# A hybrid attention kernel: its hand-set task slots replaced by a list scheduler, with attention tiles as filler

## The chip, the core and the metric

The kernel runs on one core of a Trainium2 chip. The core has a matrix engine (TensorE, PE in the profile), a vector engine (VectorE, DVE), a scalar engine (ScalarE, ACT), GpSimd (POOL) and SyncE (SP), which here issues nearly all the DMAs. Each engine works through its own instruction queue in order; semaphores tie the queues together. The metric is the device time of one execution in microseconds (us). The kernel before took 2002.72 us, the median of 3 runs from 1999.59 to 2007.79.

## The reference, cut to what matters

Everything is float32. The input is a batch of 4 images of 56 x 56 positions with 128 channels. Two layers follow each other.

```python
# layer 0: 7x7 neighbourhood attention with 4 heads of 32 channels
y    = group_norm(x)                        # 32 groups, statistics over a whole image
q,k,v = split(y @ qkv_w.T + qkv_b)
attn = softmax(q . k_window / sqrt(32) + rel_bias)   # 49 keys of each query
x    = x + (attn . v_window) @ proj_w.T + proj_b
# layer 1, on the 3136 tokens of an image
t = x.reshape(B, 3136, 128)
n = layer_norm(t)
q, k, v = exp(n @ Wq), exp(n @ Wk), n @ Wv
t = t + q @ (k.T @ v)                       # needs the sum over all tokens first
n = layer_norm(t)
t = t + spectral_filters(n) + sum(shift(n, i) @ M_u[i] for i in range(3))
```

Three dependences matter. The normalisation of layer 0 needs a whole image's statistics. The product `k.T @ v` needs every token of an image, so the second half of layer 1 starts when the last attention row of the image has passed through the first half. The spectral filters need whole images again.

## The kernel before

The program has three parts. `layers` does layer 0 and the start of layer 1. `spectral_layer` does the filters and `onto_the_rest` adds the result to the output. A second version of everything (`general`) runs only if the attention sums leave a safe range; with these inputs it does not. Only `layers` is changed.

In `layers` an image is cut into 7 rows of 8 x 56 positions, and each row into 5 query tiles (four of 96 queries and one of 64): 140 tiles for 4 images. One tile does this:

```python
def score_keys(n):                # 16 small matmuls -> 4 PSUM banks, one buffer (pool ps_s)
    t["sp"] = pools["ps_s"].tile([P, NH, 512], F32, tag="s", name="sp")
    for c in range(2):
        for h in range(NH):
            nc.tensor.matmul(t["sp"][:kn, h, c*nq:(c+1)*nq], keys_of(...)[hs], qTs[b, ty][hs, ...])

def exponentials(n):              # bias added by DVE out of PSUM, exponential by ACT in SBUF
    nc.vector.tensor_tensor(e, t["sp"][:kn, :, : 2 * nq], relb[...], ALU.add)
    nc.scalar.activation(e, e, AF.Exp)

def weigh_keys(n):                # 32 small matmuls -> half of 1 PSUM bank, one buffer (ps_o)
    t["po"] = pools["ps_o"].tile([P, 2, NQ], F32, name="po")
    for i in range(2):            # i = 0: weighted values, i = 1: the sum of the weights
        for c in range(2):
            for h in range(NH):
                nc.tensor.matmul(t["po"][hs, i, :nq], ones[:kn] if i else t["v"][:kn, c, hs], t["e"][:, h, c])

def collect_keys(n):              # DVE: reciprocal of the sums, then the product
    nc.vector.reciprocal(rec, po[:, 1, :nq])
    nc.vector.tensor_tensor(aT, po[:, 0, :nq], rec, ALU.mult)
```

All other work is written as tasks (Python generators): `group_stats` and `group_norm`, `keys`, `queries`, `values`, `mix` (projection and first half of layer 1 of a row), `products` (the 128 x 128 product of an image), `finish` (second half of a row), `row_transforms` (start of the filters), `filter_transforms` and `filter_matrices`. They share the 3 PSUM banks that the attention leaves. The main loop places them between the steps of the tiles, at tile numbers written by hand, and a task may ask to be left alone for a number of slots (`late`):

```python
for b in range(B):
    n0 = b * PER                                   # PER = 35 tiles an image
    for k in range(2, NCH):
        at(n0 + 5 * (k - 1) - 4, heads_of, b, k)   # values, queries, keys of a row
    ...
    for k in range(NCH):
        at(n0 + 5 * k + 8, lambda b, k: start(mix(b, k)), b, k)
        n1 = n0 + PER + 8
        at(n1 + (5 * k) // 2 if b + 1 < B else n0 + PER + 5, lambda b, k: start(finish(b, k)), b, k)
    ...
while n < N + behind or tasks or any(m >= n for m in plan):
    ...
    exponentials(n)
    weigh_keys(n - 1)
    slot()                        # every waiting task makes one step if a bank is free
    collect_keys(n - 1)
    score_keys(n + 1)
    slot(); slot(); slot()
    n += 1
```

The layer norm of a row, used twice a row (in `mix` and in `finish`):

```python
def normalized(acc, hn):
    for g in range(4): nc.vector.bn_stats(stats[:, g, :], acc[...])
    ...                           # 5 small DVE operations on 112 x 4 values
    nc.gpsimd.tensor_scalar(...)  # 4 small POOL operations, one a power of -0.5
    for g in range(4):            # the normalisation itself, on POOL
        nc.gpsimd.tensor_scalar(hn[...], acc[...], rstd[...], shift[...], ALU.mult, ALU.add)
```

## Time and profile before

The profiled execution spans 2005.2 us. The engines' busy time over the whole span:

| engine | busy us | share | what it does most |
|---|---|---|---|
| PE | 1746.0 | 87% | matmuls of the filters |
| PE weight loads | 1312.5 | 65% | beside the matmuls |
| DVE | 1055.1 | 53% | copies out of PSUM, attention |
| ACT | 728.2 | 36% | copies out of PSUM, exponentials |
| POOL | 346.4 | 17% | layer norms, only in the first part |

The shares are averages over parts with different limits, so the profile is best read by part. The first part (`layers`) ends where the first matmul that writes `pg` starts, at 942.4 us. Its operations for one attention tile of 96 queries, as they are on the engines:

| operation | engine | one of 96 queries (median) | all 140 tiles |
|---|---|---|---|
| scores (`sp`), 16 matmuls | PE | | 111.8 us |
| bias added (`e<-sp,relb`) | DVE | 950 ns | 125.9 us |
| exponential (`e<-e`) | ACT | 842 ns | 111.9 us |
| weighted values and sums (`po`), 32 matmuls | PE | | 162.4 us |
| reciprocal (`recs<-po`) | DVE | 748 ns | 99.6 us |
| product (`aT<-po,recs`) | DVE | 257 ns | 35.1 us |

In a view of stages every line has the stretch in us from the start of the span, its length, then for each engine the busy us and (in brackets) the number of instructions, then the granted TensorE clock as a share of full speed, the DMA share and the GB/s. In a view of waits a line names the engine, the output and the line of code that waited, then what it waited for, then the us in total, the number of times and the longest.

### The profile page before, as it was taken

What the parts mean: (1) busy time and instruction counts of PE and PEld (TensorE: products, weight loads), DVE (VectorE), ACT (ScalarE), POOL (GpSimd) and SP (SyncE); (2) the same over time, 40 slices, a digit from 0 to 9 for tenths busy, and PEclk for the clock granted to TensorE, in tenths of its full rate; (3) what the DMA queues carried; (4) which work ended last, traced back from release to release, by engine and by line L of the source; (5) the groups of instructions that cost most, each with busy time, mean ns of one, the idle gap of its engine ahead of it and who ended that gap; (6) DMA issues with size and microseconds to landing.
All of it is one profiled execution on the core that took longest, in us unless ns stands there. A gap on an engine that the chain in (4) does not pass through costs nothing.

```text
span 2005.2 us, 69052 instructions
## 1 busy us (share of the span) xinstructions
PE 1746.0 (87%) x30641; PEld 1312.5 (65%) x30641; DVE 1055.1 (53%) x2242; ACT 728.2 (36%) x1431; POOL 346.4 (17%) x626
## 2 busy tenths in 40 slices
PE   3787877988888878875999999999999999996798
PEld 2565655756665666552888888888888888884121
DVE  2666656565656555331555555555555555552232
ACT  2243322343234323313444444444444444442000
POOL 7125324532453242140000000000000000000000
PEclk7788788888788878775899999999999999998555
DMA  4553543342223223237144443444434434343986
GB/s 102 114 113 76 112 100 103 86 123 73 75 83 108 68 60 87 79 103 196 39 92 102 90 110 85 102 107 90 111 84 106 102 84 102 86 88 92 242 217 184
DMA packets 281239, 209.33 MB, mean 104 GB/s; under 512 B 102243, under 2 KB 250115, under 8 KB 280803
## 3 DMA queue, kind: packets, MB, share of 16 engines
q1 hardware_dynamic: 274266, 191.97, 39.7%
q10 hardware_dynamic: 6664, 12.85, 2.3%
q8 instruction: 243, 3.98, 0.8%
q14 instruction: 66, 0.53, 0.1%
HBM read 117.10 MB, written 87.64 MB: 102 GB/s over the span
## 4 chain that ended last, share of the span: by engine, by line
PE 50%; DMA 5%; POOL 1%; DVE 1%; issue 1%; ACT 0%; SPq 0%; ACTq 0%; POOLq 0%; DVEq 0%
PE pg L1329 19%; PE py L1349 18%; PE po L1456 3%; PE px L1310 2%; DMA z<-zd 2%; PE xx L1310 2%; PE xx L1374 2%; PE px L1374 2%; DMA out_dram<-tl 2%; PE be L736 1%; DMA v<-vd 1%; PE bk L736 0%; PE bk L688 0%; POOL hn L440 0%; POOL v L431 0%
## 5 line engine op out<-in xcount | busy, mean ns | idle before, releaser
L1339 DVE COPY gt<-pg 128x448 f32<-128x448 f32 x672 | 388.4, 620 | 344.3 <-PE pg L1329 344.3
L1339 ACT COPY gt<-pg 128x448 f32<-128x448 f32 x672 | 326.8, 540 | 396.4 <-PE pg L1329 376.7
L1329 PE MATMUL pg<-v,mats 32*128 32x112 f32 x10752 | 401.3, 285 | 22.4 <-DMA xm<-xd 12.0
L1329 PEld LDWEIGHTS pg<-v,mats 32*128 32x128 f32 x10752 | 340.1, 190 | 108.7 <-issue 98.2
L1349 PE MATMUL py<-gt,us 128*32 128x128 f32 x9408 | 373.6, 293 | 3.5 <-ACT ys L168 1.4
L1349 PEld LDWEIGHTS py<-gt,us 128*32 128x32 f32 x9408 | 299.8, 145 | 36.4 <-issue 2.7
L989 ACT ACTIVATE e<-e 126x768 f32<-126x768 f32 (+1 forms) x140 | 111.9, 799 | 225.7 <-DVE e L983 225.5
L969 PE MATMUL sp<-qT,kp 32*126 32x96 f32 (+1 forms) x2240 | 111.8, 319 | 61.5 <-DVE e L983 60.5
L969 PEld LDWEIGHTS sp<-qT,kp 32*126 32x126 f32 (+1 forms) x2240 | 87.3, 212 | 94.8 <-DVE e L983 64.0
L1456 PE MATMUL po<-z,onto 84*56 84x512 f32 x224 | 126.0, 1066 | 22.5 <-DMA z<-zd 22.5
L983 DVE TENSOR_TENSOR e<-sp,relb 126x768 f32<-126x768 f32 (+1 forms) x140 | 125.9, 900 | 27.2 <-PE sp L969 26.4
L1019 DVE RECIPROCAL recs<-po 128x96 f32<-128x96 f32 (+1 forms) x140 | 99.6, 712 | 66.9 <-PE po L1001 66.5
L1001 PE MATMUL po<-e,v_sb 126*32 126x96 f32 (+1 forms) x2240 | 82.4, 270 | 42.1 <-DVE aT L1020 22.0
L1456 PEld LDWEIGHTS po<-z,onto 84*56 84x56 f32 x224 | 31.8, 207 | 116.6 <-issue 99.0
L1001 PEld LDWEIGHTS po<-e,v_sb 126*32 126x32 f32 (+1 forms) x2240 | 50.7, 120 | 86.5 <-issue 48.0
L1465 DVE SCALAR_TENSOR_TENSOR tl<-po,hmask,tl 56x512 f32<-56x512 f32 x56 | 42.0, 750 | 107.3 <-PE po L1456 99.5
L688 PE MATMUL bk<-mu,ut 128*112 128x128 f32 x624 | 79.2, 287 | 9.7 <-ACT ut L682 7.3
L430 POOL TENSOR_SCALAR v<-v 112x4 f32<-112x4 f32 x56 | 11.2, 199 | 431.3 <-DVE v L429 429.6
L688 PEld LDWEIGHTS bk<-mu,ut 128*112 128x112 f32 x624 | 75.7, 193 | 12.1 <-ACT ut L682 9.4
L1001 PE MATMUL po<-e,ones 126*32 126x96 f32 (+1 forms) x2240 | 80.0, 266 | 0.0
L698 DVE SCALAR_TENSOR_TENSOR acc<-bk,tmask,acc 112x128 f32<-112x128 f32 x104 | 29.3, 344 | 94.1 <-PE bk L688 71.1
L404 PE MATMUL bk<-ident,hna 112*128 112x112 f32 x108 | 40.6, 424 | 30.3 <-POOL hna L440 29.8
(196 smaller groups left out, 2116.7 us busy)
## 6 DMA issues: line engine op xcount, KB each, us to landing
xd<-xs SPq DMA_DIRECT2D x112, 168.0 KB
xm<-xd SPq DMA_DIRECT2D x84, 224.0 KB
yd<-ys SPq DMA_DIRECT2D x168, 112.0 KB
yg<-yd SPq DMA_DIRECT2D x84, 224.0 KB
zd<-zs SPq DMA_DIRECT2D x84, 224.0 KB
z<-zd SPq DMA_DIRECT2D x14, 1344.0 KB
v_sb<-vpad SPq DMA_DIRECT2D x224, 63.0 KB
acc<-in_x_dram SPq DMA_DIRECT2D x28, 224.0 KB
```

Of the source, the lines that this page charges most:

```text
L688: nc.tensor.matmul(pt[:CP, g * C : (g + 1) * C], ut[:, t0 : t0 + 2 * CP - 1 : 2], mu[:, i, :], start=(i == 0), stop=(i == NAR - 1),)
L969: nc.tensor.matmul(t["sp"][:kn, h, c * nq : (c + 1) * nq], keys_of(x0, y0 + c * KH, KH)[hs], qTs[b, ty][hs, QR * x0 : QR * x0 + nq], start ...
L983: nc.vector.tensor_tensor(e.rearrange("k (h q) -> k h q", h=NH), t["sp"][:kn, :, : 2 * nq], relb[tiles[n][3]].rearrange("k h c q -> k h (c ...
L989: nc.scalar.activation(e, e, AF.Exp)
L1001: nc.tensor.matmul(t["po"][hs, i, :nq], ones[:kn] if i else t["v"][:kn, c, hs], t["e"][:, h, c], start=(c == 0), stop=(c == 1),)
L1019: nc.vector.reciprocal(rec, po[:, 1, :nq])
L1310: nc.tensor.matmul(pu[:, b].rearrange("p c m -> p (c m)"), xm[:, s, b, :], tables_of(m1)[1], start=True, stop=True,)
L1329: nc.tensor.matmul(pg[g // 2][g % 2][:, 2 * N2 * i : 2 * N2 * (i + 1)], mats[rows, 4 * n + i, :], v[rows], start=True, stop=True,)
L1339: copy(gt[:, h, :, e0 : e0 + 4, :], pg[q][h][:, : 8 * N2].rearrange("p (i m c) -> p m i c", i=4, c=2),)
L1349: nc.tensor.matmul(py[32 * j : 32 * (j + 1), slot, :], us.rearrange("p c k m -> p (c k) m")[:, NSB * (1 - c) : NSB * (5 - c), m2], gt[:, : ...
L1374: nc.tensor.matmul(pz, tables_of(m1)[2], yg[:, s * B : (s + 1) * B].rearrange("p k e -> p (k e)"), start=True, stop=True,)
L1456: nc.tensor.matmul(po[64 * q : 64 * q + H].rearrange("p b c -> p (b c)"), onto[:, s], zin[q][:, i, s], start=(s == 0), stop=(s == NS - 1),)
```

## The change

The hand-set slots go. In their place the Python code that writes the program keeps a rough clock for each engine. Every task declares before each step whether the step uses PE and how many PSUM banks it needs, and after the step how long its engines will take (`use`). `go()` picks the next step: one whose inputs are ready by that clock, steps without PE first, then by rank. The attention tiles become tasks themselves, with the worst rank (9), so that they fill the time in which no other step is ready; three of them may be under way (`AHEAD`). SyncE's DMAs are now issued in the order in which the scheduler writes them; before, only the four compute engines had a fixed order. The clock is only used to choose the order: on the chip the semaphores decide.

```diff
+            def use(*choices):
+                engine, cost = min(choices, key=lambda c: max(busy[c[0]], at[0]) + c[1])
+                busy[engine] = max(busy[engine], at[0]) + cost
+                at[0] = busy[engine] + HOP                       # HOP = 0.2
+                return engine
 ...
+            def go():
+                now = busy["PE"]
+                for t in tasks:
+                    tensor, need, gate = t[3]
+                    ready = gate() if gate else 0.0
+                    if ready is None or need > len(banks):
+                        continue
+                    ready = max([ready, t[4]] + sorted(banks.values())[:need])
+                    if ready <= now:
+                        key = (0, tensor, t[0] if tensor else ready, t[1])
+                    else:
+                        key = (1, ready, tensor, t[0], t[1])
+                    if best is None or key < best:
+                        best, chosen, when = key, t, ready
 ...
-            pinned = ph.enter_context(tc.manual_schedule(engines={E.PE, E.DVE, E.Activation, E.Pool}))
+            pinned = ph.enter_context(
+                tc.manual_schedule(engines={E.PE, E.DVE, E.Activation, E.Pool, E.SP})
+            )
```

Ranks: `borders`, `group_norm`, `products` 0; `selection`, `keys`, `queries`, `values`, `mix` 1; `group_stats`, `finish` 2; `row_transforms` 3; `regress` (the shifted products, now a task apart from `finish`) 4; the filter tasks and the range checks 5; `attend` 9.

The attention tile is changed in three ways. The exponential is taken of the scores where they stand in PSUM, and the bias comes in as a factor, `exp(bias)`, made once at the start by ACT. The scores of even and odd tiles lie in the two halves of the same four banks, and the results in two halves of one bank:

```diff
+                scores = pools["s"].tile([P, NH, 2, 256], F32, name="scores")
+                results = pools["o"].tile([P, 2, 2, NQ], F32, name="results")
 ...
+                yield pe(0, after(("qT", b, ty), *rows_of_tile("kp", n),
+                                  *when("raised", n - 2), *when("score", n - 1)))
+                sp = scores[:kn, :, n % 2, : 2 * nq]
 ...                                                   # 16 matmuls as before
+                use(("ACT", 0.9))
+                nc.scalar.activation(e.rearrange("k (h q) -> k h q", h=NH), sp, AF.Exp)
+                done("raised", n)
+                use(("DVE", 0.9))
+                nc.vector.tensor_tensor(e, e, relb[qc].rearrange("k h c q -> k (h c q)"), ALU.mult)
 ...
+                yield pe(0, after(("v_sb", n), *when("collected", n - 2), *when("weighed", n - 1)))
+                po = results[:, n % 2]
 ...                                                   # 32 matmuls as before
-                nc.vector.tensor_tensor(
-                    e.rearrange("k (h q) -> k h q", h=NH), t["sp"][:kn, :, : 2 * nq],
-                    relb[tiles[n][3]].rearrange("k h c q -> k h (c q)"), ALU.add)
-                nc.scalar.activation(e, e, AF.Exp)
```

Several steps may now run on one of two engines, whichever the rough clock has free first:

```diff
-                nc.scalar.copy(in_order(cols), as_turned(pt))
+                copy(in_order(cols), as_turned(pt), 0.55, 0.6)          # ACT or DVE
 ...
-                    nc.gpsimd.tensor_scalar(cols, cols, gmean, grstd, ALU.subtract, ALU.mult)
+                    e = nc.vector if use(("DVE", 0.5), ("POOL", 1.9)) == "DVE" else nc.gpsimd
+                    e.tensor_scalar(cols, cols, gmean, grstd, ALU.subtract, ALU.mult)
 ...                                                   # in normalized:
+                e = nc.vector if use(("DVE", 0.9), ("POOL", 1.4)) == "DVE" else nc.gpsimd
 ...                                                   # 6 small operations instead of 5
+                engine = use(("ACT", 1.3), ("POOL", 1.8))               # the normalisation itself
```

The two `row_transforms` tasks of an image now take its 14 pieces in turn (even and odd) instead of one half of the image each. The check of the attention sums is stricter and a check of the biases is added; both are a few small operations. `spectral_layer` and `onto_the_rest` are the same.

## The prediction

> **What bounds the kernel now.** I read the profile by part: first the granted clock over the span, then the busy times of five stretches, then the waits of TensorE. The lines of PE's busy tenths and of its clock in 40 slices (a slice is 50 us):
>
> ```profile
> PE   3787877988888878875999999999999999996798
> PEclk7788788888788878775899999999999999998555
> ```
>
> From slice 20 to 36 PE is full at full clock. In the first 18 slices it has gaps, and its clock stands at 7 or 8 tenths. The busy times of the stretches (head; attention of all images; tail up to the filters; filters; output):
>
> ```profile
> 0.00:38.00 38.00, 14.59 (x56) 10.31 (x56) 9.21 (x37) 8.44 (x20) 23.19 (x54) 0.73 0.42 102
> 38.00:272.00 234.00, 170.57 (x2645) 129.00 (x2645) 140.21 (x299) 71.62 (x131) 80.35 (x102) 0.78 0.48 104
> ...
> 628.00:820.00 192.00, 163.22 (x2264) 120.33 (x2252) 108.90 (x297) 67.28 (x119) 57.72 (x130) 0.84 0.28 80
> 820.00:942.00 122.00, 81.88 (x386) 50.65 (x385) 27.42 (x119) 28.05 (x53) 31.03 (x74) 0.68 0.47 131
> 942.00:1845.00 903.00, 886.52 (x20993) 741.97 (x20994) 513.70 (x881) 425.93 (x881) 0.00 (x0) 0.98 0.41 93
> 1845.00:2005.00 160.00, 129.57 (x228) 32.69 (x228) 42.68 (x57) 0.59 (x1) 0.00 (x0) 0.50 0.78 205
> ```
>
> The last two stretches, 903 + 160 = 1063 us, are code that the change leaves alone, and I count them as they are. Everything is decided in the first 942 us. Of the 782 us of attention (38 to 820) PE is busy 633, by adding its stretches (170.6 + 147.7 + 152.0 + 163.2); DVE 462, ACT 265, POOL 292. No engine is full; PE is nearest with 81%, so about 149 us of the loop are waits of PE. Who ends them, from the waits of PE in this stretch:
>
> ```profile
> PE sp L969 <- DVE e L983: 60.5, 36, 6.3
> PE bk L404 <- POOL hna L440: 29.8, 14, 5.4
> PE po L1001 <- DVE aT L1020: 22.0, 18, 4.1
> PE po L1001 <- DMA v_sb<-vpad: 16.7, 3, 10.8
> ```
>
> The reader is to see two kinds. Lines 1 and 3 are the single buffers of the attention: the next scores can't be written before DVE has added the bias, the next results not before DVE has collected the last. Line 2 is the order: PE stands in front of a transpose whose layer norm is still on POOL, with other work behind it in the queue. A list scheduler goes for the second kind, the bank halves for the first.
>
> [...] the clock is 0.78 to 0.86 in the loop and 0.98 where PE is full, and the same 16 matmuls of `po` take 0.87 us at 611.9 us of the span and 0.54 us at 617.8. [...] the small DVE operation below, normally 0.166 us, lasts to the end of the five POOL operations.
>
> ```profile
> 599.39 6.18 POOL L502 TENSOR_TENSOR acc<-acc,bproj 112x512 f32<-112x512 f32 x5
> 601.21 4.38 DVE L425 TENSOR_TENSOR v<-stats 112x4 f32<-112x4 f32 x1
> ```
>
> [...] The two halves of `scores` lie in the same banks, [...] nothing in the kernel before shares a bank in this way, so its trace can't tell.
>
> **The change, part by part.**
>
> *The tile's own work.* DVE loses the addition (0.950 us) and gains a product of the same 768 elements. Two small SBUF products take 0.16 us and the addition's own length gives about 1.04 ns an element, so 0.16 + 764 x 1.04 = 0.95 us: no gain. ACT's exponential moves from SBUF to PSUM; the same function on 512 elements takes 0.597 us out of PSUM (`ek`) and 0.629 out of SBUF (narrow tiles), so 0.842 - 0.03 = 0.81 us. Over 140 tiles that is 4 us of an engine that is not the bound. The chain of one tile stays as long as it was; what changes is that scores are released by ACT, 34% busy in the loop, and no longer by DVE, 59% busy.
>
> *PE's work.* The matmuls are the same. PE is busy 14.6 + 633 + 81.9 = 730 us in this part, at a mean clock of about 0.8. The attention alone took 111.8 + 162.4 = 274 us; with its warm durations (0.69 us for 16 score matmuls and 0.54 + 0.51 for 32 of the results, taken from the timeline; about 0.7 of it for the 28 narrow tiles) it would be 112 x 1.74 + 28 x 1.25 = 230, so 0.84 of what it took. I apply half of that gain, since the gaps won't all go: in the loop 633 x 0.92 = 582 us.
>
> *PE's waits in the loop.* The first three lines above are 112 us of the 149. I expect the order to take away most of line 2 and half of lines 1 and 3, and new waits to come (below). My choice is that PE is busy 86% of the new loop: 582 / 0.86 = 677 us, against 782. Of the 105 us gained, 51 are the clock and 54 waits.
>
> *The other engines have room.* DVE: 462 us plus 28 normalisations of `xc` at 0.5 us and some copies, less the 6 small operations where POOL takes them: about 470 of 677, 69%. ACT gets up to 56 layer norms of 1.3 us: 265 + 73 = 338, 50%. POOL loses them and `xc`.
>
> *The tail.* Before, 122 us from the last tile to the first filter matmul. Its chain shows 27 us in which seven layer norms go one after another over POOL (3.9 us each: 0.2 + 1.04 + 0.2 + 0.23 + 1.75, with gaps), two rows of `mix` done one after the other, cold matmuls (clock 0.68) and at the end 12 us of the load of `v`. Now ACT takes the 1.75 us (POOL keeps about 1.9 us a row), and only the last row of `mix` is left when the last tile ends. By steps: `mix` of the last row 13 us, `products` 2, additions 8, seven layer norms 18, store and reload 6, row transforms 21, last store and load of `v` 19: 87 us.
>
> *The head.* `xc` is normalised by DVE at about 0.5 us a row instead of 1.86 on POOL, which brings 3 us; 16 small exponentials of the bias go before ACT's first copies, which costs about as much. I keep 36 us.
>
> **Sum:** 36 + 677 + 87 = 800 us for the first part instead of 942. With 1063 unchanged: 1863 us in the trace's terms, and the median of the runs is 2.5 us below the profiled span, so 1860.
>
> **Rivals.**
>
> *A. The order is right by the rough clock and wrong on the chip.* Queues run in order, so a step placed too early blocks all behind it. Against the kernel before this adds SyncE, whose waits show up in the old trace too (84.5 us for the stores of `hn` behind the layer norm, L666), but there the order of DMAs was not that of the code. A late store could now hold back the loads of `v_sb`. Then PE would wait for DMAs as in line 4, and the loop would stay near 740 us: total about 1925.
>
> *B.[...]* The new product reads two SBUF tensors, 140 times, while POOL would be busy about a quarter of the time (292 us less 98 of layer norms and 45 of `xc`, of 677). If 1 in 4 of them waits 1 us, DVE gets 35 us more, mostly hidden at 69%; I expect 10 us of it on the path. If it comes as in the 4.38 us case, DVE gets over 100 us and bounds the loop: 720 us, total about 1905.
>
> *C. The halves are not two buffers.* [...] scores n+1 still wait for exponential n, though the scheduler thinks them free, and the results likewise for the collection. That costs wherever two tiles follow with no other work between: 0.81 + 0.95 us of wait at most a tile. If it happens for half of the tiles, about 60 us: total near 1920, less what stands in my 86%.
>
> *D. It goes as the rough clock would have it.* By the code's own numbers PE needs 12.9 us a row (361 us), 1.8 a tile (252) and 80 for the rest: 693 us, and less when warm. With PE at 94% and a tail of 75 us: 36 + 610 + 75 + 1063 = 1784.
>
> **The range.** The centre carries part of A, B and C already. One of them in full gives 1905 to 1925, two together 1960; D gives 1784. I take 1795 to 1935 for 8 in 10. Faster by over 2% means below 1963; only a blocked queue that costs all of the gain misses it: 0.86. Within 2%: 0.09. Slower by over 2% would take a new order that waits more than the old, with DMAs blocked in turn: 0.05.
>
> **What would show it.** The first matmul into `pg` starts near 800 us. The loop's clock rises from 0.78 to 0.86 to about 0.9, and PE's busy time in the first part falls from 730 to about 670. "sp <- DVE e" is gone from PE's waits; if C holds, "scores <- ACT e" stands in its place, and a wait of the results for `aT`. The exponential takes about 0.81 us, the product 0.95 with a tail of longer ones where B holds. Layer norm lines appear under ACT. The filters and the output stay at 903 and 160 us. I would be wrong if the filter stretch moved, if PE waited for `v_sb` or `ur` often, or if the tail stayed above 110 us.

## The result and the profile after

The changed kernel takes 1941.9 us (median, 1938.6 to 1947.5) against 2004.8 us of the kernel before, measured beside it: a ratio of 0.969 with a 95% interval of 0.966 to 0.973. So it is faster by 3%, in the direction predicted, but the 1860 us were 82 us too low and the time lies above the range (1795 to 1935).

The profiled execution spans 1936.9 us, a slice of the page's 40 is 48.4 us. PE's busy tenths and its clock:

```profile
PE   1787888888888998768999999999999999995898
...
PEclk9778989698988977877999999999999999998555
```

The gaps of the first part are fewer, not gone. The stretches of the changed kernel, with PE's busy time as the first figure after the length: head (to the first scores), attention (to the last collected result), tail (to the first full group of 32 filter matmuls), filters and output:

```profile
0.00:73.20 73.20, 24.98 (x114) 17.32 (x114) 26.65 (x72) 19.62 (x55) 23.52 (x45) 1.00 0.49 124
73.20:781.20 708.00, 604.93 (x8944) 456.60 (x8943) 461.33 (x1030) 307.89 (x589) 243.76 (x510) 0.85 0.40 98
781.20:874.20 93.00, 64.35 (x366) 44.55 (x365) 28.45 (x100) 31.54 (x67) 22.98 (x78) 0.78 0.53 147
874.20:1936.90 1062.70, 1016.82 (x21220) 774.50 (x21220) 556.25 (x938) 426.15 (x882) 0.00 (x0) 0.91 0.47 110
```

Cut by the same marks (the 942.4 us named above for the start of `pg` are the first full group; a few single matmuls into `pg` start at 936.6), the kernel before has 38.5, 780.9, 123.0 and 1062.8 us. So attention gained 73 us and the tail 30, the head lost 35, and the rest did not move. The waits of PE during attention:

```profile
PE scores L1136 <- ACT e L1152: 43.5, 43, 2.0
PE results L1166 <- DVE aT L1181: 32.4, 35, 4.4
```

Before, the same two waits (for the bias addition and for `aT`) were 60.5 and 22.0 us. They are 76 us now, of 103 us in which PE is idle. The 16.7 us for `v_sb`, which stood beside them before, are gone, and so are the 29.8 us behind a layer norm on POOL; what is left is one wait of 3.4 us, for a layer norm on ScalarE, in the tail.

One of these waits in the timeline (start, length, engine, operation, and in brackets the idle time before it and what ended it):

```profile
95.80 0.81 ACT L1152 ACTIVATE e<-scores 126x768 f32<-126x768 f32 x1 [0.58 <-PE scores L1136]
96.65 0.96 DVE L1156 TENSOR_TENSOR e<-e,relb 126x768 f32<-126x768 f32 x1 [0.77 <-ACT e L1152]
...
96.67 1.18 PE L1136 MATMUL scores<-qT,kp 32*126 32x96 f32 x16 [0.93 <-ACT e L1152]
```

The scores at 96.67 go into the other half of the banks, and PE still stands 0.93 us until the exponential of the tile before has read its half. Both halves lie in one tile and in the same banks; whether the program's semaphore stands for the tile or for the banks was not told apart, and a version with the halves in banks of their own was not run. The exponential and the product, and the layer norms that now appear under ACT (all executions of the first part: busy time, mean ns):

```profile
L1156 DVE TENSOR_TENSOR e<-e,relb 126x768 f32<-126x768 f32 x112 | 113.7, 1022 | 34.9 <-ACT e L1152 34.9
...
L1152 ACT ACTIVATE e<-scores 126x768 f32<-126x768 f32 x112 | 90.8, 811 | 97.5 <-PE scores L1136 88.5 <-PE results L1166 7.2 <-DVE v L499 1.0
...
L511 ACT ACTIVATE hna<-acc,v 112x128 f32<-112x128 f32 x92 | 37.8, 484 | 29.4 <-POOL v L505 29.3
```

And the head. SyncE issues its DMAs in the order of the code now; VectorE's queue runs in order as before:

```profile
32.39 4.92 SPq L192 DMA_DIRECT2D acc<-in_x_dram  x10
37.72 0.33 SPq L367 DMA_DIRECT2D raw<-in_rel_bias_dram  x1
...
43.96 0.18 DVE L1211 TENSOR_SCALAR raw<-raw 84x29 f32<-84x29 f32 x1 [19.19 <-DMA raw<-in_rel_bias_dram]
...
45.00 0.33 DVE L545 BATCH_NORM_AGGREGATE cmv<-gst 128x2 f32<-128x42 f32 x1
...
45.48 0.56 PE L549 MATMUL bk<-cmv,gmat 128*128 128x1 f32 x2 [34.48 <-DVE tmask L961]
...
48.28 1.25 DVE L571 TENSOR_SCALAR xc<-xc,gmean,grstd 128x448 f32<-128x448 f32 x2
```

The new check of the biases (`judge_bias`) has loaded nothing by the time its first operation is due: its DMA is issued at 37.7 us, behind ten loads of `x`. VectorE stands 19.2 us in front of it, and behind it in the queue is the aggregate of the group norm, for which PE stands 34.5 us and without which no key can be computed. PE's matmuls at this place, before and after (all executions of the first part: busy time, mean ns, idle time before them and what ended most of it):

```profile
L478 PE MATMUL bk<-cmv,gmat 128*128 128x1 f32 x8 | 2.3, 359 | 12.0 <-DVE tmask L822 12.0
```

```profile
L549 PE MATMUL bk<-cmv,gmat 128*128 128x1 f32 x8 | 1.7, 280 | 34.6 <-DVE tmask L961 34.5
```

**A yardstick for what follows.** The first part, up to the filter matmuls, can be split into PE's busy and PE's idle time. All kernels of the study, each by its one profiled execution, in us:

| kernel | head | attention | tail | PE busy | PE idle | clock in attention |
|---|---|---|---|---|---|---|
| before | 38.5 | 780.9 | 123.0 | 729.9 | 212.5 | 0.83 |
| after | 73.2 | 708.0 | 92.9 | 694.2 | 179.9 | 0.85 |
| HOP 0.15 | 75.5 | 715.4 | 92.4 | 705.2 | 178.1 | 0.84 |
| HOP 0.3 | 76.0 | 684.7 | 94.8 | 680.8 | 174.7 | 0.87 |
| late check | 58.6 | 699.5 | 93.9 | 692.1 | 159.9 | 0.86 |
| true gates | 74.3 | 693.2 | 89.5 | 693.1 | 163.9 | 0.88 |
| late check, true gates | 58.0 | 683.5 | 90.6 | 681.9 | 150.3 | 0.90 |
| also later rows held back | 59.3 | 686.3 | 90.6 | 694.0 | 142.2 | 0.88 |
| first tile first, true gates | 34.2 | 731.8 | 90.4 | 704.5 | 151.8 | 0.86 |
| bias added first | 74.0 | 695.4 | 91.4 | 679.7 | 181.1 | 0.87 |
| before, exponential from PSUM | 35.4 | 827.9 | 127.4 | 744.6 | 246.2 | 0.81 |
| one engine each | 76.8 | 681.9 | 98.7 | 690.1 | 167.3 | 0.87 |
| layer norm on GpSimd | 74.7 | 711.4 | 100.9 | 704.5 | 182.5 | 0.86 |
| copies and xc on one engine | 76.3 | 683.6 | 92.4 | 674.6 | 177.8 | 0.88 |
| one engine each, late, gates | 63.6 | 682.5 | 96.5 | 680.8 | 161.9 | 0.90 |
| copies and xc, late, gates | 62.1 | 671.4 | 92.1 | 685.8 | 139.9 | 0.89 |
| SyncE's order free | 73.7 | 715.9 | 93.7 | 707.0 | 176.3 | 0.84 |
| attention at rank 0 | 60.8 | 641.5 | 176.6 | 686.7 | 192.2 | 0.89 |

### The profile page after: what moved, and what is told of

The parts are those of the page before. It is cut to its first block, busy times and chain, and to the rows that moved or that the text cites. A ratio compares the mean times of both kernels' runs of the same rounds, so it can differ in the third digit from the quotient of the medians.

```text
span 1936.9 us, 69076 instructions
## 1 busy us (share of the span) xinstructions
PE 1711.1 (88%) x30641; PEld 1293.0 (67%) x30641; DVE 1072.7 (55%) x2137; ACT 785.2 (41%) x1593; POOL 290.3 (15%) x632
## 4 chain that ended last, share of the span: by engine, by line
PE 71%; DMA 11%; DVE 8%; ACT 3%; issue 2%; SPq 2%; POOL 2%; ACTq 0%; DVEq 0%; POOLq 0%
PE pg L1469 19%; PE py L1489 18%; PE results L1166 5%; PE scores L1136 4%; PE bk L862 3%; DMA out_dram<-tl 3%; PE px L1450 2%; PE po L1596 2%; PE bk L672 2%; PE bk L797 2%; DMA z<-zd 2%; PE xx L1450 2%; PE xx L1514 2%; PE px L1514 2%; ACT e L1152 2%
## 5 line engine op out<-in xcount | busy, mean ns | idle before, releaser
L1152 ACT ACTIVATE e<-scores 126x768 f32<-126x768 f32 (+1 forms) x140 | 107.5, 768 | 126.6 <-PE scores L1136 114.3
L1156 DVE TENSOR_TENSOR e<-e,relb 126x768 f32<-126x768 f32 (+1 forms) x140 | 132.5, 955 | 44.0 <-ACT e L1152 43.9
L1180 DVE RECIPROCAL recs<-results 128x96 f32<-128x96 f32 (+1 forms) x140 | 99.8, 713 | 94.5 <-PE results L1166 94.1
L1136 PE MATMUL scores<-qT,kp 32*126 32x96 f32 (+1 forms) x2240 | 112.7, 317 | 44.0 <-ACT e L1152 43.5
L1136 PEld LDWEIGHTS scores<-qT,kp 32*126 32x126 f32 (+1 forms) x2240 | 88.1, 211 | 78.0 <-ACT e L1152 58.4
L1166 PE MATMUL results<-e,v_sb 126*32 126x96 f32 (+1 forms) x2240 | 83.9, 274 | 38.4 <-DVE aT L1181 32.4
L1166 PEld LDWEIGHTS results<-e,v_sb 126*32 126x32 f32 (+1 forms) x2240 | 51.4, 121 | 88.7 <-DVE aT L1181 43.3
L456 ACT COPY xs<-bk 84x512 f32<-84x512 f32 x107 | 57.0, 583 | 75.5 <-PE bk L862 67.9
L1166 PE MATMUL results<-e,ones 126*32 126x96 f32 (+1 forms) x2240 | 80.5, 267 | 0.0
L862 PE MATMUL bk<-ur,into 28*84 28x512 f32 x224 | 75.3, 736 | 5.3 <-DMA ur<-ud 4.2
```

What stands on the lines that cost most here:

```text
L862: nc.tensor.matmul(px[wh][: 2 * N1], into[rows], ur[rows].rearrange("h w c -> h (w c)"), start=True, stop=True,)
L1136: nc.tensor.matmul(sp[:, h, c * nq : (c + 1) * nq], keys_of(x0, y0 + c * KH, KH)[hs], qTs[b, ty][hs, QR * x0 : QR * x0 + nq], start=True, ...
L1152: nc.scalar.activation(e.rearrange("k (h q) -> k h q", h=NH), sp, AF.Exp)
L1156: nc.vector.tensor_tensor(e, e, relb[qc].rearrange("k h c q -> k (h c q)"), ALU.mult)
L1166: nc.tensor.matmul(po[hs, i, :nq], ones[:kn] if i else v_sb[:kn, c, hs], e[:, h, c], start=(c == 0), stop=(c == 1),)
```

## How much is only another order

An edit of a list schedule changes the order of everything behind it. Two runs alter one number of the rough clock and no step.

```diff
-            HOP, LANDING = 0.2, 3.5
+            HOP, LANDING = 0.15, 3.5        # and, in the second, 0.3
```

> The changed kernel with one number of the rough clock altered (HOP 0.15 instead of 0.2): no step is different, but the order of steps is another one from the first tiles on. It measures what an arbitrary change of order is worth, as a yardstick for edits that alter the order too. Theory, order alone is worth little: 1936 to 1948 us. Rival, orders scatter by 10 to 25 us: outside 1930 to 1953, in either direction.

> As the one before, with HOP 0.3, another arbitrary order. Theory, order alone is worth little: 1936 to 1948 us. Rival, orders scatter: the two and the changed kernel spread by 15 us or more, and then an edit that moves the time by less than that can't be credited with it.

Measured: 1936.8 us (ratio 0.966, 0.963 to 0.969) and 1920.8 us (0.959, 0.956 to 0.962). The changed kernel and these two spread by 21 us, so the first lies in the range of its theory, and with the second the rival holds. The view of the stretches, for the first parts of the two:

```profile
0.00:883.30 883.30, 705.22 (x9421) 523.40 (x9421) 522.09 (x1201) 363.91 (x723) 287.54 (x618) 0.85 0.42 105
```

```profile
0.00:855.50 855.50, 680.83 (x9421) 514.88 (x9422) 516.82 (x1191) 359.85 (x713) 292.58 (x638) 0.87 0.44 108
```

The same 9421 matmuls take 705 us in one order and 681 in the other; the idle time is 178 and 175, and 180 in the changed kernel. The spread shows in the time of the matmuls and in the clock, hardly in the waits. Not all of it is the order: the profiled execution of HOP 0.15 was the slowest of its four (1945.7 us, the median is 1936.8), and four executions of one and the same order, that of "late check, true gates" below, run from 1893.3 us at a mean clock of 0.903 to 1911.0 us at 0.894. So an edit below is credited with time where PE's idle time moves by some 15 us or more, three times the 5 us by which these three orders differ. Three orders are few, so smaller steps stay open, and a change of the total by less than 20 us alone says nothing.

## The head and the gates

**The bias check starts later.**

```diff
                 raw = small.tile([rows, 3, BIAS_W], F32, name="raw", bufs=1)
-                yield on()
+                yield on(after(("go",)))
```

> The changed kernel with one edit: the check of the biases may start only after the attention has begun. In the changed kernel VectorE stands for 19.2 us in front of that check's DMA (issued at 37.7 us, landed at 44), and the statistics of the first image wait behind it in the same queue. Theory (a step placed by a clock that knows nothing of SyncE's earlier DMAs blocks the queue): the first scores move from 73 us to 50 to 58 us, and the median from 1942 to 1919 to 1927 us. Rival (the head is bound by the loads and stores that SyncE issues after 32 us): the first scores stay after 66 us and the median within 7 us of 1942.

Measured: 1915.3 us (0.956, 0.953 to 0.959). The first scores come at 58.6 us instead of 73.2, and PE is idle 20 us less. PE's wait for the aggregate of the group norm, 34.5 us before:

```profile
PE bk L549 <- DVE cmv L545: 9.9, 1, 9.9
```

One task of a few small operations, due too early, cost that much.

**The scheduler is told of the bank.** Scores n wait for exponential n - 1 instead of n - 2, results n for collection n - 1. In the changed kernel PE waits at these two places already, 43 times (43.5 us) and 35 times (32.4 us); the edit lets the scheduler put other steps there.

```diff
-                 *when("raised", n - 2), *when("score", n - 1)
+                 *when("raised", n - 1), *when("score", n - 1)
-                 *when("collected", n - 2), *when("weighed", n - 1)
+                 *when("collected", n - 1), *when("weighed", n - 1)
```

> The changed kernel with the scheduler told that scores of tile n wait for the exponential of tile n-1 and results of n for the collection of n-1 (it believed n-2 in both). The chip's semaphores are the same. Theory (the halves of a bank are not two buffers, and the scheduler sends PE into waits it doesn't know): PE's waits of scores for ACT (43.5 us) and of results for DVE (32.4 us) fall by half or more together, the attention loop by 20 to 35 us, the median to 1907 to 1922 us. Rival (those waits are there because no other work is ready): the waits move to other rows and the median stays within 6 us of 1942.

Measured: 1921.1 us (0.958, 0.954 to 0.963). PE's waits during attention:

```profile
PE scores L1136 <- ACT e L1152: 15.9, 20, 1.5
PE results L1166 <- DVE aT L1181: 14.5, 17, 2.4
```

From 75.9 us to 30.4. PE's idle time falls by 16 in all, since other waits take part of the room. So the halves are not two buffers in this program: declared as one, they cost less.

**Both.**

> The changed kernel with both edits of the runs before: the check of the biases after the attention has begun, and the scheduler told that scores wait for the exponential of the tile before and results for its collection. Theory (one is a cost of the head, the other of the loop, so they add: 26 + 20 us): median 1888 to 1904 us. Rival (both fill the same idle time of PE): no better than the better of the two, 1908 to 1918 us.

Measured: 1902.7 us (0.953, 0.949 to 0.956), idle 150 us. The gains nearly add: 30 us of idle time, against 20 and 16 alone.

**Keys, queries and values from the third row on also wait for attention to be open.**

```diff
+            def later(b, k):
+                return [("go",)] if b == 0 and k > 1 else []
-                yield pe(1, after(("xc", b, k)))              # keys and queries likewise
+                yield pe(1, after(("xc", b, k), *later(b, k)))
```

> Both edits of the run with late check and true gates, and in addition the keys, queries and values of rows 2 to 6 of the first image may start only once the attention may. Theory (PE does these rows of rank 1 before the first tile of rank 9, in the part where nothing else runs beside it): the first scores 8 to 14 us earlier than with the two edits alone, the median 5 to 12 us lower. Rival (the same work only moves to after the start, where PE is the bound as well): within 4 us of it.

Measured: 1896.3 us (0.946, 0.943 to 0.950), first scores at 59.3 us. The expectation of the head failed: the gate opens before the first tile is picked, and the held steps, of better rank, go first anyway. In its timeline PE also stands 5.8 us at the transposes of the second image, whose `x` is issued from 32.4 us on: again a step placed in front of its load. Idle time fell by 8 us against the version before, the total by 6, too little to credit.

**Everything that the first tile does not need waits for its scores** (with the true gates).

```diff
+                return [("score", 0)] if b == 0 and k > 1 else []
-                yield on(after(*earlier("acc", b, k, 17)))
+                yield on(after(*earlier("acc", b, k, 17), *([("score", 0)] if b else [])))
+                yield on(after(("score", 0)))     # matrices, filter tables, bias check
```

> True gates, and everything that the first tile doesn't need waits for its scores: the check of the bias, keys, queries and values from the third row on, group statistics of the second image, the choice of matrices, the filter tables. In the version with only the rows held back TensorE stood 6 us for x of the second image and 4 us for a value row behind VectorE's 5.6 us wait for a matrix. Theory, the head was lost to steps whose loads the rough clock takes for landed: first scores at 38 to 43 us (the kernel before: 38.5), and the whole at 1872 to 1885 us. Rival, the work held back comes later anyway and the loads still bound the early tiles: first scores at 38 to 43 too, but attention longer by what the head gained, 1893 to 1906 us.

Measured: 1905.2 us (0.950, 0.947 to 0.953). The first scores come at 34.2 us, even earlier than expected, and attention takes 731.8 us: in the total and in attention it is as the rival said. Against "late check, true gates" the head lost 10 us of idle time and attention gained 12. PE's longest waits in its attention (its line numbers are three or four higher), and VectorE's for the same rows:

```profile
PE results L1170 <- DVE aT L1185: 17.1, 19, 4.8
PE bk L599 <- DVE vt L652: 16.9, 1, 16.9
```

```profile
DVE vt L652 <- DMA vpad<-vt: 32.5, 12, 11.7
```

The values that were held back now wait for the stores of the rows before them; in "late check, true gates" the same wait is 17.9 us. An early first tile is thus possible, and here it was worth nothing: attention gained in waits what the head lost.

## The tile's own work

**The bias is added first, in the new order:** VectorE adds it out of PSUM, ScalarE takes the exponential in SBUF, as before the change.

```diff
-                nc.scalar.activation(e.rearrange("k (h q) -> k h q", h=NH), sp, AF.Exp)
+                nc.vector.tensor_tensor(e.rearrange(...), sp, relb[qc].rearrange(...), ALU.add)
                 done("raised", n)
-                nc.vector.tensor_tensor(e, e, relb[qc].rearrange("k h c q -> k (h c q)"), ALU.mult)
+                nc.scalar.activation(e, e, AF.Exp)
```

> The changed kernel with the bias added by VectorE out of PSUM first and the exponential taken in SBUF after it, as before the change; order by the list scheduler as it is. Theory (the scores are released sooner by ScalarE than by the busier VectorE): slower than the changed kernel by 10 to 30 us, PE's waits of scores for VectorE above 60 us, median 1952 to 1972 us. Rival (the chain of a tile is as long either way, and the scheduler fills the gap): within 6 us of 1942.

Measured: a ratio of 0.966 (0.962 to 0.970), against 0.969 (0.966 to 0.973) for the changed kernel. Idle time 181 and 180 us. One of its five executions took 2011.8 us at a mean clock of 0.78 instead of 0.89 and is left out; the other four have a median of 1932.2 us. The wait that the theory named did come, PE's for VectorE at the scores (64.6 us, where 43.5 us for ScalarE stood), but the wait of the results for `aT` fell from 32.4 to 13.5 us. So in the new order it makes no difference to the time which engine releases the scores.

**The exponential from PSUM and the product alone, in the old order** (an edit of the kernel before).

```diff
-                nc.vector.tensor_tensor(e.rearrange(...), t["sp"][:kn, :, : 2 * nq], relb..., ALU.add)
-                nc.scalar.activation(e, e, AF.Exp)
+                nc.scalar.activation(e.rearrange(...), t["sp"][:kn, :, : 2 * nq], AF.Exp)
+                nc.vector.tensor_tensor(e, e, relb..., ALU.mult)
```

> The kernel before with the exponential taken out of PSUM by ScalarE and the bias multiplied in by VectorE; the hand-set order and the single buffers stay. Theory (release by ScalarE shortens the wait of the next scores, 60.5 us in the kernel before): faster than before by 8 to 25 us, median 1980 to 1997 us. Rival 1 (order is all): within 5 us of 2004. Rival 2 [...]: slower by 10 us or more, products of over 1.5 us in the trace.

Measured: 2052.6 us, slower than the kernel before by 2.5% (1.025, 1.021 to 1.028). Only rival 2 ("slower by 10 us or more") leaves room for that much. In the kernel before it was ScalarE that waited for VectorE at this place:

```profile
ACT e L989 <- DVE e L983: 225.5, 88, 8.9
```

In this version VectorE waits for ScalarE:

```profile
DVE e L988 <- ACT e L985: 170.5, 70, 9.4
```

The wait has changed sides, from the less loaded engine (265 us of busy time in attention) to the more loaded one (462). Behind VectorE's product stand the additions and copies that other rows wait for. PE's own wait of the scores is down to 4.6 us, and still PE is idle 34 us more. Two waits grew most: in front of the results, for which the profile names no releaser (27 times, 61.4 us; before, no such line), and for a layer norm on POOL, from 29.8 us:

```profile
PE bk L406 <- POOL hna L442: 64.0, 24, 4.6
PE po L1002 <- issue: 61.4, 27, 6.5
```

That these waits come from VectorE's fits the list; no run isolates it. Rival 2 is not excluded either. The longest of its 140 products took 7.41 us, where the median is 0.96; what held it up is not shown. VectorE is busy 461 us in attention in both kernels, so its busy time does not hold the 50 us. But POOL, with about as many operations (494 and 498), is busy 322 us in attention instead of 291, and that may lengthen the layer norms that PE waits for. The list schedule pays nothing for the same edit.

## One engine or two, filler and SyncE

Five runs give back the choice of engine.

```diff
-                if use(("ACT", act), ("DVE", dve)) == "ACT":          # copies
+                if use(("ACT", act)) == "ACT":
-                e = ... if use(("DVE", 0.9), ("POOL", 1.4)) == "DVE" else ...   # layer norm factors
+                e = ... if use(("DVE", 0.9)) == "DVE" else ...
-                e = ... if use(("DVE", 0.5), ("POOL", 1.9)) == "DVE" else ...   # xc
+                e = ... if use(("POOL", 1.9)) == "DVE" else ...
-                engine = use(("ACT", 1.3), ("POOL", 1.8))             # the normalisation
+                engine = use(("POOL", 1.8))
```

**All four in the changed kernel.**

> The changed kernel with the choice of engines taken back: copies by ScalarE, the layer norm's small operations by VectorE and its normalisation by GpSimd, the group normalisation by GpSimd, as before the change; the scheduler knows it. Theory (part of the gain is the layer norm off GpSimd, in the tail above all): slower than the changed kernel by 15 to 45 us, median 1957 to 1987 us, and the tail from the last collection to the first filter matmul above 105 us. Rival (the scheduler hides GpSimd's time behind attention tiles): within 8 us of 1942.

Measured: 1921.3 us (0.961, 0.958 to 0.964), outside both expectations: it is 20 us faster. The tail is 6 us longer (98.7), not above 105. PE is idle 167 us, 13 less than in the changed kernel, and its wait for POOL at the transposes of `hna`, line 2 of the prediction, is 3.9 us in the whole first part.

**Only the normalisation on GpSimd.**

> The changed kernel, where only the normalisation itself (1.3 or 1.8 us a row by the rough clock) has GpSimd alone again; copies, factors and xc keep their choice of two. Together with those, one engine took 20.5 us off. Theory: ScalarE's layer norms (92 + 72 instructions, about 80 us of it) stand in front of exponentials[...]; so most of the gain is here: 1920 to 1928 us, the wait of the scores for ScalarE falls from 43.5 us to under 30, the tail grows by 5 to 8 us. Rival: the gain came from the copies and xc in VectorE's queue; then this one is 1938 to 1950 us, with the longer tail.

Measured: 1947.1 us (0.973, 0.970 to 0.976), the tail 8 us longer, as the rival had it. The wait of the scores for ScalarE is 38.7 us, not under 30.

**Only the other three.**

> The changed kernel, where the copies out of PSUM have ScalarE alone, the layer norm factors VectorE alone and the normalisation of xc GpSimd alone; the normalisation of the layer norm keeps its choice of two. Theory (layer norms on ScalarE are what costs): 1935 to 1945 us, the waits of the scores for ScalarE stay near 43 us or grow. Rival (VectorE's queue is what costs, its xc at 0.97 us each instead of the declared 0.5 among it): 1918 to 1928 us, and the waits of the results for aT fall below 25 us.

Measured: 1916.8 us (0.959, 0.956 to 0.961), in the range of the rival. But its wait of the results for `aT` did not fall below 25 us (35.2), and of its 22 us in the first part PE's busy time makes 20 and the idle time 2. By the yardstick above no wait was taken away, and the gain can't be told from another order.

**All four, with late check and true gates.**

> The changed kernel with three edits together: the check of the bias starts with the first scores, the gates of scores and results know of the bank (one tile back), and copies, layer norm factors, layer norms and the normalisation of xc have one engine each. Late check and true gates together gave 1902.7 us, one engine alone took 20.5 us off the changed kernel. Theory, separate causes: the gains add, 1878 to 1890 us, first scores near 59 us, attention near 665 us, tail near 90 us. Rival, the choice of engine and the gates cure the same waits (both are about the order of steps in VectorE's and ScalarE's queues): 1894 to 1905 us, attention near 682 us.

Measured: 1913.0 us (0.957, 0.954 to 0.959), above both ranges and not faster than with late check and true gates alone (1902.7; 0.953, 0.949 to 0.956); idle 162 us against 150. The gains do not add, as the rival said.

**The three without the normalisation, with late check and true gates.**

> Late check of the bias, true gates, and copies on ScalarE, factors on VectorE, xc on GpSimd; the layer norm keeps its choice of two. Late check and gates gave 1902.7, copies and xc on one engine alone took 25 us off the changed kernel, and with the layer norm on GpSimd too nothing was left of that. Theory, VectorE's queue is a cause of its own: 1876 to 1888 us, attention near 660 us. Rival, the 25 us were the same waits that the true gates remove, or the luck of one order: 1895 to 1912 us.

Measured: 1892.3 us (0.944, 0.938 to 0.949). It lies between the two ranges. It is the fastest kernel of the study, 2.6% below the changed one by the ratios; the step against "late check, true gates" (10 us of the time, 10 us of idle time) is within what an order alone moves. The last two versions differ only in where the normalisation may go, and by 22 us of idle time in favour of the choice. Elsewhere the same choice does not do that: in the changed kernel it is worth 3 us of idle time (180 against 182.5), and with the other three given back it costs 10 (178 against 167). What holds in all three pairs is the tail, shorter by 8, 6 and 4 us. So the choice for the layer norm is worth something in the tail; what it does in the loop depends on the rest of the order, and for the other choices these runs show nothing. Why all four given back together have 13 us less idle time, and neither part alone, stays open.

**Attention at rank 0 instead of 9.**

```diff
-                    start(9, attend(n + AHEAD))
+                    start(0, attend(n + AHEAD))
```

> The changed kernel, with the attention tiles at rank 0 instead of 9: they go whenever they are ready, and the rest fills. Theory, the filler matters: tiles run one after another with nothing between,[...] and the steps of mix, finish and the row transforms pile up behind; attention ends sooner but the tail grows beyond 130 us: 1955 to 2010 us; the scores' wait for ScalarE goes above 70 us. Rival, rank hardly counts, because at most three tiles are under way and each is soon waiting for its own chain, so that the others go anyway: 1925 to 1950 us, with the first scores at 60 us or before.

Measured: 1940.7 us (0.969, 0.965 to 0.973), the same as with rank 9, as the rival had it in total. In its parts it was neither: attention is 67 us shorter, the tail 84 longer as the theory said, and the wait that grew is that of the results, not of the scores:

```profile
PE results L1166 <- DVE aT L1181: 91.9, 81, 5.6
PE scores L1136 <- ACT e L1152: 7.8, 9, 4.7
```

So the rank keeps work for the gaps, but in this kernel it decides only where the waiting is done, not when the kernel ends.

**SyncE's order left free.**

```diff
-    engines={E.PE, E.DVE, E.Activation, E.Pool, E.SP}
+    engines={E.PE, E.DVE, E.Activation, E.Pool}
```

> The changed kernel with SyncE's order left to the framework, as before the change; the four compute engines keep the scheduler's order. Theory (PE hardly waits for a DMA in the loop, so the order of DMAs carries neither gain nor loss there, and the head stays as it is since VectorE's queue still has the check of the biases in front): within 12 us of 1942. Rival (DMAs in the scheduler's order are what makes the new order run): slower by 20 us or more, with waits of PE for v_sb or ur.

Measured: 1946.1 us (0.972, 0.968 to 0.975), as with the fixed order. The head is the same too (73.7 us), so it was not the fixed order of SyncE that cost it.

## Where the prediction failed, and what of it held

The sum was 36 + 677 + 87 = 800 us for the first part. Measured: 73 + 708 + 93 = 874, with the rest unchanged at 1062.7. So of the 82 us the head has 37, the loop 31 and the tail 6; the last 7.5 us are the median, which was taken to lie 2.5 us below the profiled span and lies 5 above it.

- **The head** is the step that failed most, 73 us instead of 36. "I keep 36 us" weighed costs of engine time (the exponentials of the bias, the normalisation of `xc`, which took VectorE 0.97 us a row on average and not 0.5) and not the order in which the queues meet the loads. The bias check was described as "a few small operations" and left out of the step; it blocked VectorE 19 us. PE's idle time in the head is 48 us where the kernel before had 24, and 10 us more PE work lie in it (25.0 against 14.6), which is moved, not lost. The late check brought 20 us of idle time back.
- **PE's work in the loop** is the second: 605 us busy instead of 582, 23 of the 31 us. The step gave all matmuls of the loop 0.92 of their time, half of what the attention's own matmuls would gain at their shortest. Just these did not get shorter. The scores before and after:

```profile
L969 PE MATMUL sp<-qT,kp 32*126 32x96 f32 (+1 forms) x2240 | 111.8, 319 | 61.5 <-DVE e L983 60.5
```

```profile
L1136 PE MATMUL scores<-qT,kp 32*126 32x96 f32 (+1 forms) x2240 | 112.7, 317 | 44.0 <-ACT e L1152 43.5
```

The results took 133.9 us before and 136.4 after, with the overlap of their two groups counted once. (The 162.4 us of the first table, and so the 274 and the 230 us of the prediction, count it twice; this hardly changes their ratio.) What fell most is the transposes in front of which the layer norm used to stand:

```profile
L404 PE MATMUL bk<-ident,hna 112*128 112x112 f32 x108 | 40.6, 424 | 30.3 <-POOL hna L440 29.8
```

```profile
L469 PE MATMUL bk<-ident,hna 112*128 112x112 f32 x112 | 22.9, 335 | 9.9 <-DVE vt L649 6.1 <-ACT hna L511 3.4
```

In the whole first part PE's busy time fell by 36 us instead of 60, to 694, and the loop's clock rose to 0.85, not to about 0.9. Eight versions that share the head and the gates of the changed kernel have 675 to 707 us, so 670 was not reached by any of them. That matmuls are shorter at a higher clock is in the trace before: 16 matmuls of `po` took 0.87 us where the clock was 0.50 (611.5 to 613.5 us of the span) and 0.54 us where it was 1.00 (617.5 to 619.5 us). That fewer gaps bring the higher clock, on which the step rests, was an estimate and is not shown: in "late check, true gates" the loop is idle 89 us, its clock 0.90 and its busy time 594 us, but with true gates alone it is idle 86 us and busy 608, and in "bias added first" it is idle 104 us, as in the changed kernel (103), and busy 592. What sets the clock in the loop stays open.
- **PE's waits in the loop** are the smaller part, 103 us where the step left 95, but two errors meet in them. "Half of lines 1 and 3" would have left 41 of 82.5 us; 75.9 stayed. This is rival C: by the 43 + 35 waits the halves act as one buffer in this trace. The text had C as a rival ("for half of the tiles, about 60 us") and only part of it in the centre. Its sum is loose: 70 tiles at 0.81 + 0.95 us are up to 123 us, not 60. On the other side the remaining waits, 66 us before, fell to 27 and not to the 54 that the step leaves. Line 2, the queue behind the layer norm, went as predicted, from 29.8 us to 3.4, and by the order, as predicted: with the normalisation on POOL again it stays at 3.9 us ("one engine each") and 4.7 ("layer norm on GpSimd").
- **Busy 86%** of the loop was right (605 of 708), by two errors that cancel in the quotient: more busy time and more waits.
- **The tail** was right in what it consists of: 93 us against 87, with layer norms on ScalarE; these alone are 8 of the 30 us that it gained.
- **The tile's work** was right: 0.81 us for the exponential. The product takes 0.95 us in the median and 1.02 on average, 1.87 at most; over 112 tiles that is 8 us of VectorE, so rival B, an estimate from one operation of 4.38 us, is small in the changed kernel. **Rival A** came true in VectorE's queue in the head, not for SyncE and `v_sb`. (Of its evidence, the 84.5 us of L666 end in the profile with a copy of `ut` on POOL; 52.5 us more end with the layer norm.) A in the head and C in the loop came together, for which the text had "two together 1960"; the range allowed for one of them only.

**What made the kernel faster.** Between the two traces PE is busy 36 us less and idle 33 us less: 45 us less in the loop and 12 in the tail, 24 more in the head. Each of these parts of the change, taken back alone, leaves the gain about as it was (ratios of 0.959 to 0.973): the exponential out of PSUM, the choices of engine, the rank of the tiles, SyncE's order. The tile's edit alone, in the old order, loses 2.5%, and the halves acted as one buffer (75.9 us of waits). What remains is the order of the list itself. This is by elimination: the parts were not taken back together, and two smaller ones (row transforms in turn, the shifted products as a task of their own) not at all.

## What to carry to other kernels

A schedule made ahead of time is as good as its model of what blocks: give it the buffers that the semaphores guard (here both halves of the banks together, by the 43 + 35 waits, not each half) and the state of the DMA queue at its start, and look in the first 80 us of the trace for a small operation that waits long in a queue others need. Compare two list schedules by TensorE's idle time too, and alter an arbitrary number of the scheduler a few times to learn what another order is worth before crediting an edit. When moving a step to another engine, ask which of the two will then do the waiting.

## What the runs showed of the hardware

In this kernel the clock does not follow from how busy PE is. In the version with attention at rank 0, two stretches of the tail, both with PE over 95% busy:

```profile
725.00:775.00 50.00, 47.74 (x325) 32.73 (x324) 26.12 (x99) 20.73 (x43) 22.64 (x69) 1.00 0.67 187
800.00:850.00 50.00, 48.68 (x130) 18.12 (x126) 4.35 (x8) 21.45 (x41) 0.00 (x0) 0.50 0.80 219
```

The same matmul of 28 rows in each of them:

```profile
L862 PE MATMUL bk<-ur,into 28*84 28x512 f32 x60 | 15.9, 617 | 0.0
```

```profile
L862 PE MATMUL bk<-ur,into 28*84 28x512 f32 x88 | 42.0, 1078 | 1.5 <-DMA ur<-ud 0.8 <-DVE vtr L458 0.7
```

It takes 0.62 us among other matmuls, at a clock of 1.00, and 1.08 us where hardly anything else runs on PE, at a clock of 0.50. The stretches in which the clock falls and rises again, and an earlier one:

```profile
750.00:762.50 12.50, 10.44 (x68) 6.90 (x68) 7.99 (x40) 5.77 (x13) 11.34 (x34) 1.00 0.75 213
...
775.00:787.50 12.50, 12.29 (x83) 8.50 (x83) 3.72 (x11) 4.84 (x9) 0.00 (x0) 1.00 0.84 237
787.50:800.00 12.50, 8.98 (x43) 4.20 (x43) 2.76 (x7) 3.68 (x7) 0.00 (x0) 0.85 0.80 220
800.00:812.50 12.50, 12.50 (x35) 4.80 (x32) 1.19 (x2) 5.62 (x11) 0.00 (x0) 0.50 0.79 218
...
900.00:912.50 12.50, 12.50 (x275) 10.80 (x277) 5.79 (x11) 5.18 (x11) 0.00 (x0) 0.78 0.12 39
912.50:925.00 12.50, 12.50 (x324) 11.11 (x319) 7.88 (x14) 6.16 (x13) 0.00 (x0) 1.00 0.30 36
```

The clock falls between 787.5 and 800 us, where PE is idle 3.5 of 12.5 us. From 750 to 762.5 us it was idle 2.1 us and the clock stayed at 1.00. From 800 to 812.5 us PE is busy throughout at 0.50, and the clock is back at 1.00 only from 912.5 us on. Whether it is the 28 rows or something else in that stretch was not told apart.
